# Issuing the end of attention's last block in steps within the next image's scans

## The chip, the cores and the metric

The kernel runs on one core of a Trainium2 chip. The metric is the device time of one execution in microseconds (us), lower is better; the time given is the median of several runs. A profile is one execution recorded by the hardware profiler; times in its views are us from the start of its span.

## The reference

Four images of 48 x 48 tokens with 128 channels go through two layers, each added to its input. All is float32.

```
x = x + ssm(groupnorm(x))          # layer 0: 2-D selective scan
t = tokens(x)                      # 2304 tokens of 128 channels
t = t + attention(layernorm(t))    # softmax(t t^T) t
t = t + stu(layernorm(t))          # spectral filters, 16 of them
```

Layer 0 projects each token to 256 channels and a gate, convolves them 3 x 3, and runs a linear recurrence over the tokens in four directions, with 16 states to a channel:

```
dA = exp(dt * A);  h = h * dA + (dt * u) * B;  y = sum_n h * C
```

The four y are summed, normalised, gated and projected back. Attention follows: scores, exponential, weighted sum, division by the sum of weights. The last part ("stu") is a causal convolution of the normalised tokens with 16 filters, at four lengths, mixed by weights, with a projection for each filter.

## The kernel before

**Phases.** The program does one image after the other (the loop at L1121). For image b it runs `scans` (the recurrence of b), then `epilogue` (normalise, gate, project: the input T of attention), then `attention`. The stu part of image b is not done there: it is the generator `stu`, which is drawn in small pieces inside the scans of image b + 1, and alone at the end for the last image. Likewise the prologue of image b + 1 and the first pieces of its scans' preparation (`begin_scans`) are drawn inside the attention of image b.

**Order.** Every engine (PE, DVE, ACT, POOL, and SP for DMAs) works its instructions in the order in which the Python code issues them; the order is written out by hand with generators that yield between steps. Tiles come from pools with a fixed number of buffers, and a tile that reuses a buffer waits for the last use of the former.

**Scans.** An image's recurrence has 24 chunks (4 directions by 6 stretches of 384 tokens), each with 8 units (2 halves of the channels by 4 groups of states). A unit's state tile s (pool of 6) holds 4 groups of 384 columns. For each unit: PE spreads B into a PSUM bank (L442); DVE multiplies it with rep, the loaded dt·u, into s (L450; for three units of eight POOL does this, with a loaded row of B, `bc`); ACT forms dA and DVE scans, four times (L455, L458); POOL copies the carry (L466) and multiplies by C, also a `bc` row (L467); PE sums over the states into the bank y (L475), and DVE adds that to the image's sum. In `scans` the steps of neighbouring units are interleaved: `enter`, `spread`, `prepare` (a step of a later chunk's preparation), `scan`, and `more`, which draws stu pieces until their columns keep pace.

**DMA at the turning.** `begin_scans` issues on SP, during the attention of the image before, the first chunk's dtdud stores, its rep loads (L402) and its six `bc` rows of four pieces each (L429). stu then issues, at its first draw, four filter tiles `tt` (L942), and for each of its five blocks of rows ux (L1001, L1002), mue (L1004), `res`, the tokens to which the result is added (L1006, from the tensor td), and G (L953) for each filter. ACT takes the first two `cv` results of a filter by a copy to Q (L983).

**Attention.** Blocks of queries J are taken in the order 0, 4, 1, 2, 3 (L698). For each block, 18 tiles of keys: scores on PE (L714), exponential on ACT (L716), values on PE into the bank o (L707). When a block is complete, its `tail` begins, a generator in steps:

- DVE copies o to oT (L857); PE turns it (otr, L861);
- DVE forms the denominators (den, L864 to L867) and adds the result to T (L871, L872);
- SP stores T to the tensor td in DRAM (L874);
- the layer norm of stu, `normed`: DVE sum, mean and difference (L151 to L153), ACT square (L154), DVE variance (L156, L157), POOL power (L158), DVE product into u (L160), and us from u (L886);
- PE turns u (utr, L890), ACT copies it to uT (L893), SP stores that to the tensor ud (L895).

One step of the oldest tail is taken per tile of keys. After the last tile of the last block, what is left is run to its end at once:

```
        while es:
            values()
        for t in tails:
            for _ in t:
                pass
```

The driver then closes attention's pools, opens those of the next scans, and calls `scans`.

Of the kernel before, what the change touches and what calls it, by code (L numbers as in the profile page):

```python
# [8 lines left out]
F32 = mybir.dt.float32  # L9
# [6 lines left out]
P = 128  # L16
B, H, W, C = 4, 48, 48, 128
# [4 lines left out]
CS = 384  # L22
SUB = 384
NT = L // P
# [30 lines left out]
def hybrid_kernel(ctx: ExitStack, tc: tile.TileContext, a: dict, out: bass.AP):  # L55
# [453 lines left out]
    def scans(b, chunks, preps, front, sp, back, work, work_cols):  # L509

        units = [Unit(ch, h, q) for ch in chunks for h, q in quads]
        total = len(chunks) * CHUNK_COLS + work_cols
        done = [0]

        def more(share):

            while done[0] < share * total:
                cols = next(work, None)
                if cols is None:
                    break  # L520
                done[0] += cols

        def enter(s):

            if s + 2 < len(units) and units[s + 2].pool:
                units[s + 2].enter(sp.s)
            if 0 <= s + 1 < len(units) and not units[s + 1].pool:
                units[s + 1].enter(sp.s)

        def spread(s):  # L530
            if s < len(units) and not units[s].pool:
                units[s].spread(back.psB)
                done[0] += CS

        def prepare(s):

            ci, j = divmod(s, len(quads))
            for c in range(ci + 1, ci + 4):
                if c < len(chunks) and 0 <= s - len(quads) * c + LEAD < STEPS:
                    done[0] += next(preps[c]) or 0  # L540

        def refill(s, i):

            if 0 <= s < len(units) and s // len(quads) + 1 < len(chunks):
                u, nxt = units[s], chunks[s // len(quads) + 1]
                if u.h == NH - 1:
                    nxt.fetch(i + u.q, front)

        pending = []
        spread(0)  # L550
        enter(-2)
        enter(-1)
        spread(1)
        for s in range(len(units) + 2):
            real = s < len(units)
            enter(s)
            prepare(s)
            if real:
                units[s].scan(0, back.psa)
            more((s + 0.25) / len(units))  # L560
            if 1 <= s <= len(units):
                units[s - 1].times_c()
            if real:
                units[s].scan(1, back.psa)
            if pending:
                pending.pop().add_y()
            prepare(s)
            more((s + 0.5) / len(units))
            spread(s + 2)
            if real:  # L570
                units[s].scan(2, back.psa)
            more((s + 0.75) / len(units))
            prepare(s)
            if real:
                units[s].scan(3, back.psa)
            refill(s - 3, Q4)
            if s + 1 < len(units) and units[s + 1].pool:
                refill(s + 1, 0)
            if s >= 2:
                units[s - 2].sum_c(back.psy)  # L580
                done[0] += CS
                if units[s - 2].q == Q4 - 1:
                    pending.append(units[s - 2])
            more((s + 1) / len(units))
        for u in pending:
            u.add_y()
        assert next(work, None) is None
# [3 lines left out]
    def epilogue(b, T, xn, xnT, tmp, pool, ps):  # L591
# [13 lines left out]
        def load_z(J):  # L605
            n = P * PIECES[J]
            zr[J] = tmp.tile([P, NH, 512], F32, tag=f"zr{J}", name=f"zr{b}_{J}")
            nc.sync.dma_start(zr[J][:, :, :n], zs[:, :, at(J)].rearrange("h p t -> p h t"))
            nc.sync.dma_start(T[:, 4 * J:4 * J + PIECES[J]], tokens(a["x"][b], J))

        def means(J):
            n = P * PIECES[J]
# [40 lines left out]
        def add(J, j0):  # L653
            if j0 >= PIECES[J]:
                return
            p = o.pop((J, j0))
            for f in range(2):
                t = T[:, 4 * J + j0 + f]
                nc.vector.scalar_tensor_tensor(t, p[:, 0, f], rd[J][:, j0 + f:j0 + f + 1], t, ALU.mult, ALU.add)
            t = T[:, 4 * J + j0:4 * J + j0 + 2]  # L660
            nc.vector.tensor_tensor(t, t, p[:, 1], ALU.add)

        def norm(J):
            if J not in lns:
                n = PIECES[J]
                sq = pool.two.tile([P, 4, C], F32, tag="ln_sq", name=f"asq{b}_{J}")[:, :n]
                lns[J] = normed(T[:, 4 * J:4 * J + n], xn[:, 4 * J:4 * J + n], 1e-5, pool.two, sq, f"a{b}_{J}")
            next(lns[J], None)

        def turned(J):  # L670
# [15 lines left out]
                    stage(slot - s)  # L686
                    yield slot - s if stage is kept else None

    def attention(b, T, xn, xnT, pool, tmp, ps):

# [2 lines left out]

        pieces = [0, 4, 1, 2, 3]  # L698
        slots = [(J, i) for J in pieces for i in range(NT)]
        es, po, tails = [], {}, []  # L700

        def values():
            J, i, e = es.pop(0)
            w = P * PIECES[J]
            if i == 0:
                po[J] = ps.two.tile([P, 512], F32, tag="o", name=f"o{b}_{J}")
            nc.tensor.matmul(po[J][:, :w], xn[:, i], e[:, :w], start=(i == 0), stop=(i == NT - 1))  # L707
            if i == NT - 1:
                tails.append(tail(b, J, T, po.pop(J), tmp, ps))

        for J, i in slots:
            w = P * PIECES[J]
# [9 lines left out]
            yield  # L722
        while es:
            values()
        for t in tails:
            for _ in t:
                pass
# [119 lines left out]
        for t in us[b]:  # L847
            nc.gpsimd.memset(t[KP[-1]:, NM - 1], 0.0)

    def tail(b, J, T, po, pool, ps):  # L850


        u, sums = us[b]
        n, k = PIECES[J], KP[J]
        T = T[:, 4 * J:4 * J + n]
        oT = pool.two.tile([P, 512], F32, tag="oT", name=f"oT{b}_{J}")
        nc.vector.tensor_copy(oT[:, :P * n], po[:, :P * n])  # L857
        yield
        p = ps.two.tile([P, 4, C], F32, tag="tr", name=f"otr{b}_{J}")[:, :n]
        for j in range(n):  # L860
            nc.tensor.transpose(p[:, j], oT[:, j * P:(j + 1) * P], ident)  # L861
        yield
# [11 lines left out]
        nc.sync.dma_start(tokens(td, J), T)  # L874
        x = T
        if n < 4:

# [2 lines left out]
            nc.sync.dma_start(x[:k], td[512 * J:].rearrange("(p j) c -> p j c", j=4))  # L880
            for i in range(3):
                yield
        sq = pool.one.tile([P, 4, C], F32, tag="sq", name=f"usq{b}_{J}")
        for _ in normed(x[:k], u[:k, J], 1e-5, pool.two, sq, f"u{b}_{J}"):
            yield
        nc.vector.tensor_tensor(sums[:k, J], u[:k, J, 0:2], u[:k, J, 2:4], ALU.add)  # L886
        yield
        p = ps.two.tile([P, 512], F32, tag="tr", name=f"utr{b}_{J}")[:, :4 * k]
# [3 lines left out]
        uT = pool.two.tile([P, 4 * P], F32, tag="uT", name=f"uT{b}_{J}")[:, :4 * k]  # L892
        nc.scalar.copy(uT, p)  # L893
        yield
        nc.sync.dma_start(ud[:, :, 1 + P * J:1 + P * J + k], uT.rearrange("c (j p) -> c j p", j=4))  # L895
# [4 lines left out]
    def stu(b, pool, ps):  # L900
# [95 lines left out]
        def begin(n):  # L996
            (lo, hi, place, extra), k = items[n]
            m = 2 if extra else 1

            now["x"] = pool.one.tile([P, 6, P], F32, tag="ux", name=f"ux{b}_{n}")  # L1000
            nc.sync.dma_start(now["x"][:, 2:, :hi - lo], ud[:, :, 1 + lo:1 + hi])  # L1001
            nc.sync.dma_start(now["x"][:, :2, :hi - lo], ud[:, 2:, lo:hi])  # L1002
            now["mu"] = pool.one.tile([P, 2, 3, C], F32, tag="mue", name=f"mue{b}_{n}")
            nc.sync.dma_start(now["mu"][:, :m], mud[:, place:place + m])  # L1004
            now["T", n] = pool.two.tile([P, 4, C], F32, tag="res", name=f"res{b}_{n}")
            nc.sync.dma_start(now["T", n][:hi - lo], td[4 * lo:4 * hi].rearrange("(p j) c -> p j c", j=4))  # L1006

        def parts(w, extra):

# [40 lines left out]
            yield 4 * w  # L1050

        def ended(n, p, lo, hi):
            t = now.pop(("T", n - KF + 1))[:hi - lo]
# [4 lines left out]
        for n, (_, k) in enumerate(items):  # L1058
            if k == 0:
                begin(n)  # L1060
            for c in range(3):
                for g in range(2):
                    yield from conv(n, c, g)
# [54 lines left out]
    first = begun(begin_scans(0, front))  # L1118
    begin0.close()
    start_y(0)  # L1120
    for b in range(B):  # L1121
        sp = Stage(tc, f"h{b}", "left", s=(6, SB))
        ps = Stage(tc, f"b{b}", "right", psa=(2, PSUM), psy=(1, PSUM), psB=(1, PSUM), psc=(3, PSUM), psp=(1, PSUM))
        bank["mm"] = ps.psB, "B"
        if b == 0:
            mixed = Stage(tc, "m", "right", two=(2, SB))
            scans(b, *first, front, sp, ps, mixture(mixed, ps), MIX_COLS)
            mixed.close()
        else:
            scans(b, *first, front, sp, ps, stu_alone(b - 1, ps), STU_COLS)  # L1130
        ps.close()
        sp.close()
        front.close()
        turn = Stage(tc, f"t{b}", "left", one=(1, SB))
        back = Stage(tc, f"a{b}", "right", one=(1, SB), two=(2, SB), four=(4, SB))
        T = back.one.tile([P, NT, C], F32, tag="T", name=f"T{b}")
        xn = back.one.tile([P, NT, C], F32, tag="xn", name=f"xn{b}")
        xnT = back.one.tile([P, L], F32, tag="xnT", name=f"xnT{b}")
        begin_stu(b)
# [4 lines left out]
        at = attention(b, T, xn, xnT, back, back, ps)  # L1144
# [85 lines left out]
```

## Time and profile before

| | |
|---|---|
| time, 3 runs | 6412.86, 6416.79, 6426.66 us; median 6416.79 |
| span of the profile | 6421.2 us, 75575 instructions |
| mean granted TensorE clock | 0.919 |
| PE, DVE, ACT, POOL busy | 85%, 75%, 44%, 60% |
| DMA | 1033.52 MB, mean 161 GB/s |
| attention of image 0 to scans of image 1: last `o` copied, first scan, first `cv` | 1450.73, 1471.49, 1473.78 us |
| the same, images 1 to 2 | 2887.72, 2908.48, 2910.63 us |
| the same, images 2 to 3 | 4317.93, 4338.69, 4340.76 us |

How to read it: the busy shares are averages over phases with different limits, so what happens at one place has to be read from the timeline there. A line in the timeline gives start, duration, engine, line of the kernel, operation, the tiles written and read, and in brackets how long the engine had been idle and what ended that.

### The profile page before, as it was taken

Reading aid. Unit: us, or ns where it says so; the run is one execution under the profiler, and the core shown is the slowest. Engines: PE = TensorE matmul, PEld = TensorE weight load, DVE = VectorE, ACT = ScalarE, POOL = GpSimd, SP = SyncE. Lnnn points to the kernel's source line nnn. Section 1 sums busy time; section 2 is a strip of 40 time slices with the busy share of each in tenths; the row PEclk is TensorE's granted clock in tenths of the full one; section 3 lists DMA queues with packets and bytes.
Section 4 is the critical chain, followed back from the end, with each engine's and each line's share of the span. In section 5 each row is a group of like instructions: output and inputs, shape, how many; then the busy total and the mean of one; then the engine's idle time right before and its main releaser. Section 6 shows DMA issues by size and latency. Waiting matters only on the chain.

```text
span 6421.2 us, 75575 instructions
## 1 busy us (share of the span) xinstructions
PE 5440.6 (85%) x25032; PEld 3353.1 (52%) x25032; DVE 4823.6 (75%) x6193; ACT 2800.0 (44%) x5053; POOL 3842.7 (60%) x1825
## 2 busy tenths in 40 slices
PE   3656555697999998888999999788999999789999
PEld 1222222444556566544556567544555567547789
DVE  6999999548999998558999998458999999322111
ACT  2555555244555554244555554244555554221000
POOL 1989888406778887306788887207788888100000
PEclk6787777799999999899999999899999999899999
DMA  4556566126878889127878889127788888025546
GB/s 104 139 138 151 139 144 148 40 55 162 199 196 215 216 221 247 59 62 165 198 195 217 222 218 256 39 64 179 189 203 215 219 224 246 28 67 151 154 141 212
DMA packets 658246, 1033.52 MB, mean 161 GB/s; under 512 B 93856, under 2 KB 515872, under 8 KB 633120
## 3 DMA queue, kind: packets, MB, share of 16 engines
q1 hardware_dynamic: 652032, 1025.00, 62.3%
q10 hardware_dynamic: 5824, 3.69, 0.3%
q8 instruction: 200, 3.28, 0.2%
q14 instruction: 190, 1.56, 0.1%
HBM read 905.79 MB, written 122.56 MB: 160 GB/s over the span
## 4 chain that ended last, share of the span: by engine, by line
PE 45%; DVE 24%; DMA 16%; POOL 4%; issue 4%; ACT 4%; SPq 3%; DVEq 0%; ACTq 0%; POOLq 0%
PE cv L969 19%; DVE s L458 11%; PE pr L1031 6%; DVE s L450 5%; DMA tt<-fd 5%; DMA rep<-dtdud 4%; PE s L714 4%; PE y L475 3%; PE o L707 3%; DMA bc<-xdd 3%; POOL s L467 3%; PE op L650 2%; PE B L442 2%; DVE xc L264 2%; DVE re L408 2%
## 5 line engine op out<-in xcount | busy, mean ns | idle before, releaser
L467 POOL TENSOR_TENSOR s<-s,bc 128x1536 f32<-128x1536 f32 x768 | 2647.8, 3449 | 179.8 <-DVE s L458 88.9
L458 DVE TENSOR_TENSOR_SCAN s<-dA,carry,s 128x384 f32<-128x384 f32 x2560 | 2458.1, 1000 | 190.1 <-ACT dA L455 189.0
L455 ACT ACTIVATE dA<-rep,A 128x384 f32<-128x384 f32 x3072 | 1782.0, 585 | 1627.0 <-DVE s L458 1622.2
L969 PE MATMUL cv<-tt,u 128*128 128x256 f32 (+3 forms) x7680 | 1632.6, 351 | 64.3 <-DVE U L994 38.0
L969 PEld LDWEIGHTS cv<-tt,u 128*128 128x128 f32 x7680 | 1259.7, 190 | 583.1 <-issue 266.1
L450 POOL TENSOR_TENSOR s<-rep,bc 128x1536 f32<-128x1536 f32 x288 | 994.2, 3452 | 95.3 <-DMA bc<-xdd 95.3
L969 PE MATMUL cv<-tt,us 128*128 128x256 f32 (+3 forms) x3840 | 841.0, 358 | 106.6 <-DVE U L994 55.3
L994 DVE TENSOR_TENSOR U<-cv,Q 128x256 f32<-128x256 f32 (+1 forms) x1280 | 480.3, 381 | 596.0 <-PE cv L969 581.2
L450 DVE TENSOR_TENSOR s<-rep,B 128x1536 f32<-128x1536 f32 x480 | 832.2, 1734 | 56.1 <-PE B L442 32.8
L475 PE MATMUL y<-s,csum 128*32 128x384 f32 x6144 | 720.6, 544 | 142.4 <-DVE ya L481 85.0
L969 PEld LDWEIGHTS cv<-tt,us 128*128 128x128 f32 x3840 | 639.7, 195 | 323.8 <-DVE U L994 89.7
L1031 PE MATMUL pr<-U,G 128*128 128x512 f32 (+4 forms) x2048 | 694.7, 469 | 3.5 <-DVE U L994 3.2
L983 ACT COPY Q<-cv 128x256 f32<-128x256 f32 (+3 forms) x640 | 224.0, 351 | 1027.2 <-PE cv L969 1025.5
L442 PE MATMUL B<-xd,spread 128*128 128x384 f32 x960 | 443.0, 546 | 177.4 <-DVE s L450 166.8
L458 DVE TENSOR_TENSOR_SCAN s<-dA,s 128x384 f32<-128x384 f32 x512 | 459.3, 938 | 70.9 <-ACT dA L455 70.7
L466 POOL COPY carry<-s 128x4 f32<-128x4 f32 x640 | 121.6, 190 | 574.8 <-DVE s L458 534.5
L1031 PEld LDWEIGHTS pr<-U,G 128*128 128x128 f32 x2048 | 334.5, 190 | 198.2 <-issue 137.0
L714 PE MATMUL s<-xnT 128*128 128x512 f32 (+1 forms) x720 | 357.9, 582 | 42.7 <-ACT xnT L676 23.4
L475 PEld LDWEIGHTS y<-s,csum 128*32 128x32 f32 x6144 | 127.7, 112 | 497.4 <-issue 336.3
L158 POOL TENSOR_TENSOR ln_vu<-ln_vu,mhalf 128x4 f32<-128x4 f32 (+1 forms) x20 | 26.8, 1341 | 602.0 <-DVE ln_vu L157 602.0
L716 ACT ACTIVATE e<-s,shift 128x512 f32<-128x512 f32 (+1 forms) x360 | 231.2, 644 | 314.1 <-PE s L714 313.6
L707 PE MATMUL o<-e,xn 128*128 128x512 f32 (+1 forms) x720 | 343.4, 560 | 4.5 <-ACT e L716 4.5
(157 smaller groups left out, 3638.1 us busy)
## 6 DMA issues: line engine op xcount, KB each, us to landing
rep<-dtdud SPq DMA_DIRECT2D x768, 384.0 KB, 7.8
tt<-fd SPq DMA_DIRECT2D x192, 577.0 KB, 5.5
bc<-xdd SPq DMA_DIRECT2D x2304, 48.0 KB, 3.4
tt<-fd SPq DMA_DIRECT2D x192, 513.0 KB, 4.5
tt<-fd SPq DMA_DIRECT2D x192, 385.0 KB, 4.3
dtdud<-re SPq DMA_DIRECT2D x768, 96.0 KB, 2.3
G<-gd SPq DMA_DIRECT2D x192, 256.0 KB, 5.3
tt<-fd SPq DMA_DIRECT2D x64, 514.0 KB, 5.6
```

Source lines behind the costliest of these rows:

```text
L442: nc.tensor.matmul(self.bt[:, :CS], spread[:, self.ch.k // 2, self.q].rearrange("p c j -> p (c j)"), self.ch.xd, start=True, stop=True)
L450: eng.tensor_tensor(s, self.ch.rep[self.h][:, 1], bt.unsqueeze(1).to_broadcast([P, G4, CS]), ALU.mult)
L455: nc.scalar.activation(dA[:, :CS], ch.rep[self.h][:, 0, g], AF.Exp, scale=A[:, ch.k, self.h * G4 + g, self.q:self.q + 1])
L458: nc.vector.tensor_tensor_scan(s, dA[:, CS - 1::-1] if ch.rev else dA[:, :CS], s, 0.0 if ch.first else carry[:, self.h, self.q, g:g + 1], ...
L467: nc.gpsimd.tensor_tensor(self.s, self.s, ch.bc[Q4 + self.q].unsqueeze(1).to_broadcast([P, G4, CS]), ALU.mult)
L475: nc.tensor.matmul(ch.y[g * DL:(g + 1) * DL, :CS], csum, self.s[:, g], start=(self.q == 0), stop=(self.q == Q4 - 1))
L707: nc.tensor.matmul(po[J][:, :w], xn[:, i], e[:, :w], start=(i == 0), stop=(i == NT - 1))
L714: nc.tensor.matmul(p[:, :w], xnT[:, i * P:(i + 1) * P], xnT[:, 512 * J:512 * J + w], start=True, stop=True)
L716: nc.scalar.activation(e[:, :w], p[:, :w], AF.Exp, bias=shift)
L969: nc.tensor.matmul(p2[:, :, at - first:], x, t[:, :, hi - 1 - at + J * P:end if end >= 0 else None:-1], start=(J == 0), stop=(J == nb - 1))
L994: nc.vector.tensor_tensor(dst, src, q, ALU.add)
L1031: nc.tensor.matmul(p[:, :, :v], Gs[n][:, q, x, :], U[n][:, 4 * q:4 * q + 4, :v], start=False, stop=(k == KF - 1 and q == 1 and v == w))
```

## The change

The last block of attention (J = 3) of each image but the last keeps its tail as a generator. Only its first step, the copy to oT, is issued within attention. The others are issued from within `scans` of the next image by `attend()`: one ahead of the first `spread`, two after the first scan of unit 0, and then one at a time up to the middle of unit 2. Such a tail uses the bank y for its two transposes, and a tile of the state pool as scratch for the square and for uT; its small tiles lie in a pool that stays open. T of that block lies in the slot of u that the norm will fill. Its store to td is issued by ACT in place of SP, in a step of its own. T is one tile per block in place of one for all; `begin_stu`, which takes the tiles u and us and clears their last rows, comes ahead of the other tiles. In stu, `res` is loaded at the block's fourth filter (k = 3) in place of the first, and has one buffer in place of two.

```
+        def attend(n=1):
+            for i in range(n):
+                if last_tail and next(last_tail[0], True):
+                    last_tail.pop()
+
+        if last_tail:
+            bank["scratch"] = sp.s.tile([P, G4, CS], F32, tag="s", name=f"sc{chunks[0].name}").rearrange("p g t -> p (g t)")
+        attend()
         spread(0)
         enter(-2)
         enter(-1)
         spread(1)
...
                 units[s].scan(0, back.psa)
+            attend(2 if s == 0 else 1)
             more((s + 0.25) / len(units))
...
             prepare(s)
+            attend()
             more((s + 0.5) / len(units))
             spread(s + 2)
             if real:
                 units[s].scan(2, back.psa)
+            if s:
+                attend()
             more((s + 0.75) / len(units))
...
+            if s == 0:
+                attend()
             more((s + 1) / len(units))
```

```
         while es:
             values()
+        if rest is not None:
+            last_tail.append(tails.pop())
+            next(last_tail[0])
         for t in tails:
             for _ in t:
                 pass
...
-        nc.sync.dma_start(tokens(td, J), T)
+        (nc.scalar if scratch else nc.sync).dma_start(tokens(td, J), T)
+        if scratch:
+            yield
...
-        sq = pool.one.tile([P, 4, C], F32, tag="sq", name=f"usq{b}_{J}")
+        if scratch:
+            sq = bank["scratch"][:, :4 * C].rearrange("p (j c) -> p j c", c=C)
+        else:
+            sq = pool.one.tile([P, 4, C], F32, tag="sq", name=f"usq{b}_{J}")
...
-            now["T", n] = pool.two.tile([P, 4, C], F32, tag="res", name=f"res{b}_{n}")
-            nc.sync.dma_start(now["T", n][:hi - lo], td[4 * lo:4 * hi].rearrange("(p j) c -> p j c", j=4))
+
+        def load_T(n):
+            (lo, hi, place, extra), k = items[n]
+            now["T"] = pool.one.tile([P, 4, C], F32, tag="res", name=f"res{b}_{n}")
+            nc.sync.dma_start(now["T"][:hi - lo], td[4 * lo:4 * hi].rearrange("(p j) c -> p j c", j=4))
...
             if k == 0:
                 begin(n)
+            elif k == 3:
+                load_T(n)
...
+        rest = Stage(tc, f"r{b}", "right", one=(1, SB), two=(1, SB)) if b + 1 < B else None
+        begin_stu(b)
...
-        T = back.one.tile([P, NT, C], F32, tag="T", name=f"T{b}")
+
+        T = [us[b][0][:, J] if rest and J == PIECE_ORDER[-1] else
+             back.one.tile([P, n, C], F32, tag=f"T{J}", name=f"T{b}_{J}") for J, n in enumerate(PIECES)]
```

More of the change, by code (lines that the diff above doesn't have):

```diff
@@ L549, in scans, with attend @@
         pending = []
+        def attend(n=1):
+            for i in range(n):
+                if last_tail and next(last_tail[0], True):
+                    last_tail.pop()
+        if last_tail:
+            bank["scratch"] = sp.s.tile([P, G4, CS], F32, tag="s", name=f"sc{chunks[0].name}").rearrange("p g t -> p (g t)")
+        attend()
         spread(0)
@@ L559, in scans @@
                 units[s].scan(0, back.psa)
+            attend(2 if s == 0 else 1)
             more((s + 0.25) / len(units))
@@ L567, in scans @@
             prepare(s)
+            attend()
             more((s + 0.5) / len(units))
@@ L571, in scans @@
                 units[s].scan(2, back.psa)
+            if s:
+                attend()
             more((s + 0.75) / len(units))
@@ L583, in scans @@
                     pending.append(units[s - 2])
+            if s == 0:
+                attend()
             more((s + 1) / len(units))
@@ L608, in load_z @@
             nc.sync.dma_start(zr[J][:, :, :n], zs[:, :, at(J)].rearrange("h p t -> p h t"))
-            nc.sync.dma_start(T[:, 4 * J:4 * J + PIECES[J]], tokens(a["x"][b], J))
+            nc.sync.dma_start(T[J], tokens(a["x"][b], J))
         def means(J):
@@ L657, in add @@
             for f in range(2):
-                t = T[:, 4 * J + j0 + f]
+                t = T[J][:, j0 + f]
                 nc.vector.scalar_tensor_tensor(t, p[:, 0, f], rd[J][:, j0 + f:j0 + f + 1], t, ALU.mult, ALU.add)
-            t = T[:, 4 * J + j0:4 * J + j0 + 2]
+            t = T[J][:, j0:j0 + 2]
             nc.vector.tensor_tensor(t, t, p[:, 1], ALU.add)
@@ L666, in norm @@
                 sq = pool.two.tile([P, 4, C], F32, tag="ln_sq", name=f"asq{b}_{J}")[:, :n]
-                lns[J] = normed(T[:, 4 * J:4 * J + n], xn[:, 4 * J:4 * J + n], 1e-5, pool.two, sq, f"a{b}_{J}")
+                lns[J] = normed(T[J], xn[:, 4 * J:4 * J + n], 1e-5, pool.two, sq, f"a{b}_{J}")
             next(lns[J], None)
@@ L687, in epilogue, with attention @@
                     yield slot - s if stage is kept else None
-    def attention(b, T, xn, xnT, pool, tmp, ps):
-        pieces = [0, 4, 1, 2, 3]
+    def attention(b, T, xn, xnT, pool, tmp, ps, rest):
+        pieces = PIECE_ORDER
         slots = [(J, i) for J in pieces for i in range(NT)]
@@ L708, in values @@
             if i == NT - 1:
-                tails.append(tail(b, J, T, po.pop(J), tmp, ps))
+                kept_ = rest is not None and J == pieces[-1]
+                tails.append(tail(b, J, T[J], po.pop(J), rest if kept_ else tmp,
+                                  last_bank if kept_ else lambda name: ps.two.tile([P, 512], F32, tag="tr", name=name), kept_))
         for J, i in slots:
@@ L848, in begin_stu, with last_bank, tail @@
             nc.gpsimd.memset(t[KP[-1]:, NM - 1], 0.0)
-    def tail(b, J, T, po, pool, ps):
+    PIECE_ORDER = [0, 4, 1, 2, 3]
+    last_tail = []
+    def last_bank(name):
+        pool, tag = bank["tail"]
+        return pool.tile([P, 512], F32, tag=tag, name=name)
+    def tail(b, J, T, po, pool, mm_tile, scratch):
         u, sums = us[b]
         n, k = PIECES[J], KP[J]
-        T = T[:, 4 * J:4 * J + n]
         oT = pool.two.tile([P, 512], F32, tag="oT", name=f"oT{b}_{J}")
@@ L858, in tail @@
         yield
-        p = ps.two.tile([P, 4, C], F32, tag="tr", name=f"otr{b}_{J}")[:, :n]
+        p = mm_tile(f"otr{b}_{J}").rearrange("p (j c) -> p j c", c=C)[:, :n]
         for j in range(n):
@@ L887, in tail @@
         yield
-        p = ps.two.tile([P, 512], F32, tag="tr", name=f"utr{b}_{J}")[:, :4 * k]
+        p = mm_tile(f"utr{b}_{J}")[:, :4 * k]
         for j in range(4):
@@ L891, in tail @@
         yield
-        uT = pool.two.tile([P, 4 * P], F32, tag="uT", name=f"uT{b}_{J}")[:, :4 * k]
+        uT = (bank["scratch"] if scratch else pool.two.tile([P, 4 * P], F32, tag="uT", name=f"uT{b}_{J}"))[:, :4 * k]
         nc.scalar.copy(uT, p)
@@ L1052, in ended @@
         def ended(n, p, lo, hi):
-            t = now.pop(("T", n - KF + 1))[:hi - lo]
+            t = now["T"][:hi - lo]
             nc.vector.tensor_tensor(t, t, p[:hi - lo], ALU.add)
@@ L1120, in hybrid_kernel @@
     start_y(0)
+    rest = None
     for b in range(B):
@@ L1124, in hybrid_kernel @@
         bank["mm"] = ps.psB, "B"
+        bank["tail"] = ps.psy, "y"
         if b == 0:
@@ L1130, in hybrid_kernel @@
             scans(b, *first, front, sp, ps, stu_alone(b - 1, ps), STU_COLS)
+        assert not last_tail
         ps.close()
@@ L1133, in hybrid_kernel @@
         front.close()
+        if rest:
+            rest.close()
+        rest = Stage(tc, f"r{b}", "right", one=(1, SB), two=(1, SB)) if b + 1 < B else None
+        begin_stu(b)
         turn = Stage(tc, f"t{b}", "left", one=(1, SB))
         back = Stage(tc, f"a{b}", "right", one=(1, SB), two=(2, SB), four=(4, SB))
-        T = back.one.tile([P, NT, C], F32, tag="T", name=f"T{b}")
+        T = [us[b][0][:, J] if rest and J == PIECE_ORDER[-1] else
+             back.one.tile([P, n, C], F32, tag=f"T{J}", name=f"T{b}_{J}") for J, n in enumerate(PIECES)]
         xn = back.one.tile([P, NT, C], F32, tag="xn", name=f"xn{b}")
         xnT = back.one.tile([P, L], F32, tag="xnT", name=f"xnT{b}")
-        begin_stu(b)
         more = b + 1 < B
@@ L1143, in hybrid_kernel @@
         bank["mm"] = ps.one, "mm"
-        at = attention(b, T, xn, xnT, back, back, ps)
+        at = attention(b, T, xn, xnT, back, back, ps, rest)
         slots = NT * len(PIECES)
```

## The prediction

> **What bounds the kernel now.** I read the page first: the tenths of each engine, then the chain. No engine binds everywhere; the chain runs through PE for 45% and DVE for 24%.
>
> ```profile
> PE   3656555697999998888999999788999999789999
> DVE  6999999548999998558999998458999999322111
> ...
> PE 45%; DVE 24%; DMA 16%; POOL 4%; issue 4%; ACT 4%; SPq 3%; DVEq 0%; ACTq 0%; POOLq 0%
> ```
>
> So I went to the place of the change. There are three turnings from an image's attention to the next image's scans. In the timeline of the first (columns: start, us, engine, line) everything after the last `o` matmul hangs on one serial thread:
>
> ```profile
> 1450.73 0.68 DVE L857 COPY oT<-o 128x512 f32<-128x512 f32 x1
> 1451.47 0.65 PE L861 MATMUL otr<-ident,oT 128*128 128x128 f32 x4 [1.19 <-DVE oT L857]
> ...
> 1454.44 0.34 SPq L874 DMA_DIRECT2D td<-T  x1
> ...
> 1458.77 3.42 POOL L450 TENSOR_TENSOR s<-rep,bc 128x1536 f32<-128x1536 f32 x1
> 1458.83 3.90 DVE L160 TENSOR_TENSOR u<-u,ln_vu 128x512 f32<-128x512 f32 x1 [1.19 <-POOL ln_vu L158]
> ...
> 1464.64 1.65 PE L442 MATMUL B<-xd,spread 128*128 128x384 f32 x2 [0.68 <-ACT uT L893]
> 1466.32 1.75 DVE L450 TENSOR_TENSOR s<-rep,B 128x1536 f32<-128x1536 f32 x1 [3.13 <-PE B L442]
> ...
> 1468.16 4.17 SPq L942 DMA_DIRECT2D tt<-fd  x4
> ...
> 1471.49 1.80 DVE L458 TENSOR_TENSOR_SCAN s<-dA,s 128x384 f32<-128x384 f32 x2
> ...
> 1473.78 2.08 PE L969 MATMUL cv<-tt,us 128*128 128x256 f32 x4 [4.01 <-DMA tt<-fd]
> ...
> 1475.04 0.37 ACT L983 COPY Q<-cv 128x256 f32<-128x256 f32 x1 [9.47 <-PE cv L969]
> ```
>
> Call the start of oT O. The first scan comes at O+20.8 and the first `cv` at O+23.05; in the second and third turning (O at 2887.72 and 4317.93) the first `cv` is at O+22.9 and O+22.8. Two threads start the scans: the tail with B and the state products, and SP's queue, which must bring `tt` before ACT's Q copy, behind which the third dA waits. So SP's queue and what it waits for (us, times, longest) come next:
>
> ```profile
> 1428.25 20.68 SPq L429 DMA_DIRECT2D bc<-xdd  x24
> ...
> 1449.70 0.57 SPq L386 DMA_DIRECT2D xdd<-xd  x1
> ```
> ```profile
> SPq L429 <- DMA rep<-dtdud: 11.3, 8, 1.6
> ```
> ```profile
> 4308.81 7.75 SPq L429 DMA_DIRECT2D bc<-xdd  x17
> ```
>
> A bc load shares no data with rep, yet waits for it eight times. [...] Freed of rep (the third turning), 17 pieces take 7.75 us, 0.456 each.
>
> [...] L160 takes 3.90 us beside POOL's 3.42 us L450, with a median of 0.693 otherwise. [...] here a B takes 1.65 us after the tail against 0.81 later.
>
> **The change, part by part.**
>
> *Taken out.* The tail from otr to the ud store no longer stands ahead of B. If nothing else moved, PE would do otr at O+0.74 to 1.39, then B 0.85, product 1.75, B 0.85, product 1.75 with handovers of about 0.05: first scan at O+6.75, 14.0 us earlier.
>
> *The wait put in.* The td store moves from SP to ACT. The changed kernel, built but not run, shows its order and waits, the same at all three turnings:
>
> ```
> ACT  td<-u             waits DVE (T done), DMAHW0
> SP   bc row 3, piece 1 waits DMAHW6
> SP   bc row 3, piece 2 waits DMAHW7
> SP   bc row 3, piece 3 waits DMAHW0
> ```
>
> The value that piece 3 waits for on DMAHW0 is reached only when ACT's td has landed. [...] SP, which passed these pieces from 1433 on, now stops at the seventh. Behind it on SP: 18 bc pieces, block 2's ud store, xdd, four dtdud, then `tt`, ux and mue; waiting for them are POOL's products, PE's first `cv`, and through Q all later dA and scans.
>
> When td lands: first scan O+6.75 to 7.7; den, four operations, 1.06 us (1452.16 to 1453.22) and T, five operations, 1.2 (to 1454.41): O+9.95. ACT's issue and landing aren't in the trace for td; SP's td lands in 1.7 to 2.5 us, median 2.0, and ACT's only comparable issue row is 0.59 us long. I take 2.2 with the handover, and 0.35 for B's that are partly slow (0 to 0.84 each): td lands at O+12.5 (11.8 to 14.3).
>
> Then SP: 18 pieces at 0.456 are 8.2 us (7.0 at 0.39, which is 20.68 less the 11.3 waited, over 24; 11.9 at 0.66, halfway to the 0.86 beside rep, which has long landed by then). ud and xdd 0.66 each with gaps, four dtdud 2.6 with gaps: 4.0. `tt` goes out at O+24.7, against O+17.4 before; with the same 5.65 us to the first `cv` it comes at O+30.3: **7.4 us later than before** (5.4 to 12).
>
> *Added to DVE within the first two units.* den and T lie ahead of td and are in the sum; the Q wait hides nothing more of them. The rest stands between the fourth scan of unit 0 and the third of unit 1: L151 0.72, L152 0.20, L153 0.71, L156 0.72, L157 0.20, L160 0.70, L886 0.45 with gaps: 3.7 us. The new pow on POOL is followed by a carry copy and a 3.45 us L467 product; [...] one of them is likely to sit behind it: 3.3 us (0 to 3.3). DVE had 3.4 us idle there before (the first scan of unit 2 waits for dA at 1488.05, because ACT waits for xd, xp, pr and mue). So that scan comes at +7.4+3.7+3.3−3.4 = +11.0, while PE, which must do utr after L160, is at +8.5 (+7.4, plus L151 to L160, 3.3 with gaps, less the 2.2 it waited for mue at 1481.37). DVE has idle shares behind this point (busy 9.44 of 10 from 1490 to 1500), so I let the difference close mostly: **+9 us per turning**.
>
> *Costed at nothing, each hidden by:* otr's four transposes (PE waits for O anyway); utr's and uT (0.6 us each, counted in PE's lag); the new wait of L153 for td's landing (landed 20 us before); the ud store from the scratch tile on SP, which waits for uT and has rep x4 of the second chunk behind it (issued at 1481.91 before, now some 17 us later, still landing, at 9.1 us, more than 10 us ahead of the scan at 1525 plus the delay); unit 4's state taking the scratch tile's buffer (two units later than the store); y's first sum (after uT). T in five tiles and block 3's in u's slot: the loads wait for the same end of the spectral filter. The memsets keep their place on POOL. `res` at k = 3 and in one buffer: 20 issues of 0.43 us move on SP; the stores they wait for were issued two or more filters earlier, and `res` doesn't stand in the chain. Dropping it from the start of a block could give mue up to 1 us, 0 to 5 in all; I take 0.
>
> *Sum.* Three turnings of +9: +27 us, on the profile's span of 6421.2. The runs shown are 6412.86 to 6426.66, median 6416.79; I put the difference on the median: **6444 us**. The bounds per turning are +3 (quick store, pieces at 0.39, [...] some later idle used up) and +15 (the slow ends): +9 to +45.
>
> **Rivals.**
>
> 1. *SP isn't held* (the other side). If piece 3 doesn't wait for td, SP has done xdd at 1450.3 and `tt` goes out near O+2.2; the first scan is 14.0 earlier, den and T put 2.3 back, the other DVE work 3.6 net of the idle: −8.1 per turning, −24 in all, 6393. It decides at one place: whether bc's 24 pieces run through from 1428 to 1449. For it: the tail's data need no bc. Against it: the wait in the built order, and the eight waits on rep[...]. It holds too if the steps do just what the change says.
> 2. *Held, but mostly made good.* DVE's scans wait 259.7 us for dA over the whole run; if the first chunk swallows the added work and catches up, +3 per turning: 6426, within what can't be told apart. For it: DVE's idle shares in the first units. Against: PE and DVE go in lockstep at 9 tenths after 1490.
> 3. *Held, with more behind it.* The late `tt`, ux, mue and dtdud crowd rep of the second chunk, whose load lands late; +15 per turning: 6462. For it: DMA busy share is 0.96 from 1470 to 1490. Against: the slack of over 10 us counted above.
>
> **How the numbers follow.** A measurement of this kernel tells about 0.2% (12.8 us) from no change: 6404 to 6430. My forecast (held, +5 to +13 per turning) has 0.72, rival 3 0.10, rival 2 0.10, rival 1 0.08. So slower 0.82, same 0.10, faster 0.08. The forecast and rival 3's nearer part lie within 6424 to 6462; what is left out is rival 1, part of 2 and of 3.
>
> **What would show it.** Right: SP's bc<-xdd broken after six pieces until td lands, near O+12.5; first scan near O+7, but the first `cv` near O+30; a long ACT wait before Q; L160 or L886 at about 3.9 us. Wrong: bc unbroken, first `cv` before O+15, or a DVE that has caught up by unit 8 of the first chunk.

## The result, and the profile after

| | before | after |
|---|---|---|
| time, median of 4 runs | 6414.82 us (6405.95 to 6426.66) | 6452.49 us (6450.70 to 6455.69) |
| ratio | | 1.0058, 95% interval 1.0041 to 1.0076 |
| span of the profile | 6421.2 us | 6449.9 us |
| first scan after the copy to oT, first turning | O+20.8 | O+7.2 |
| `tt` issued | O+17.4 | O+24.9 |
| first `cv` | O+23.05 | O+30.9 |

The change made the kernel 0.6% slower: 37.7 us by the medians, 12.6 a turning (a turning is the passage from one image's attention to the next one's scans; there are three). In the changed kernel's numbering oT is L885, the td store L902, `us` L919, ud L928, `tt` L975, `cv` L1002, Q L1016.

The timeline of the changed kernel at the first turning (start, us, engine, line; O is 1449.13; SPq and ACTq are the queues on which SP and ACT issue DMAs):

```profile
1449.13 0.68 DVE L885 COPY oT<-o 128x512 f32<-128x512 f32 x1
...
1456.37 0.95 DVE L458 TENSOR_TENSOR_SCAN s<-dA,s 128x384 f32<-128x384 f32 x1
...
1459.49 0.33 ACTq L902 DMA_DIRECT2D td<-u  x1
1461.51 8.19 SPq L429 DMA_DIRECT2D bc<-xdd  x18
1464.00 3.42 POOL L450 TENSOR_TENSOR s<-rep,bc 128x1536 f32<-128x1536 f32 x1 [39.97 <-DMA bc<-xdd]
...
1474.03 4.37 SPq L975 DMA_DIRECT2D tt<-fd  x4
...
1480.04 2.08 PE L1002 MATMUL cv<-tt,us 128*128 128x256 f32 x4 [25.38 <-DMA tt<-fd]
...
1481.35 0.37 ACT L1016 COPY Q<-cv 128x256 f32<-128x256 f32 x1 [32.88 <-PE cv L1002]
...
1483.05 0.96 DVE L458 TENSOR_TENSOR_SCAN s<-dA,s 128x384 f32<-128x384 f32 x1 [22.73 <-ACT dA L455]
...
1491.97 3.79 POOL L467 TENSOR_TENSOR s<-s,bc 128x1536 f32<-128x1536 f32 x1
1492.51 3.54 DVE L919 TENSOR_TENSOR us<-u 128x256 f32<-128x256 f32 x1
...
1493.44 1.04 PE L1002 MATMUL cv<-tt,us 128*128 128x256 f32 x4
1495.97 2.64 DVE L458 TENSOR_TENSOR_SCAN s<-dA,s 128x384 f32<-128x384 f32 x3
1496.95 0.58 ACT L455 ACTIVATE dA<-rep,A 128x384 f32<-128x384 f32 x1 [3.16 <-DVE s L458]
...
1497.94 0.65 ACT L1016 COPY Q<-cv 128x256 f32<-128x256 f32 x2
...
1498.37 0.70 PE L1002 MATMUL cv<-tt,u 128*128 128x256 f32 x2 [3.89 <-ACT Q L1016]
```

The first scan does come 13.5 us earlier. But 18 pieces of bc start only 2.0 us after ACT has issued td, though SP had passed them by 1449 in the kernel before. I call this stop of SP the hold. POOL has stood idle for 40 us when they let its first product start, PE 25 us when `tt` lets it start the first `cv`, ACT 33 us when it gets that `cv`, and DVE, two scans into unit 0, waits 22.7 us for ACT. SP's waits in the same stretch (us, times, longest) name what held it:

```profile
SPq L429 <- DMA td<-u: 23.6, 1, 23.6
```

On the page of the changed kernel the same shows as idle time (last column: us, what ended most of it). The rows are POOL's product with a bc row and PE's first `cv` group; before, they waited 95.3 us (bc) and 106.6 us:

```profile
L450 POOL TENSOR_TENSOR s<-rep,bc 128x1536 f32<-128x1536 f32 x288 | 994.2, 3452 | 213.7 <-DMA bc<-xdd 212.5
...
L1002 PE MATMUL cv<-tt,us 128*128 128x256 f32 (+3 forms) x3840 | 839.2, 357 | 161.6 <-DMA tt<-fd 100.0
```

**A measure for each turning.** To follow a delay further than the first units, I use the start of the first scan of unit 15 (the second chunk's last), counted from O, in the timelines. Before, it is at O+117.39, 117.17 and 116.48 in the three turnings; in the changed kernel at O+130.13, 130.64 and 129.59: 12.7, 13.5 and 13.1 later, 39.3 in all. That accounts for the 37.7 us of the medians. The scan in the first turning, before and changed:

```profile
1568.12 1.01 DVE L458 TENSOR_TENSOR_SCAN s<-dA,carry,s 128x384 f32<-128x384 f32 x1
```
```profile
1579.26 1.01 DVE L458 TENSOR_TENSOR_SCAN s<-dA,carry,s 128x384 f32<-128x384 f32 x1
```

The table gives the same for all kernels. The experiments ran in three groups; each time is beside the median of before on the same chip (6414.37, 6415.45 and 6414.71 us).

| kernel | `tt` issued, first turning | unit 15 against before, three turnings | sum | median, us | less its before | ratio, 95% interval |
|---|---|---|---|---|---|---|
| changed | O+24.9 | +12.7, +13.5, +13.1 | +39.3 | 6452.49 | +37.7 | 1.0058 (1.0041 to 1.0076) |
| e1_td_sp | O+10.8 | -0.8, -0.4, +0.1 | -1.2 | 6418.19 | +3.8 | 1.0006 (0.9999 to 1.0012) |
| e2_before_td_act | O+19.4 | +4.0, +0.3, +1.2 | +5.5 | 6413.08 | -1.3 | 1.0001 (0.9993 to 1.001) |
| e3_us_pool | O+24.9 | +6.8, +7.0, +7.3 | +21.1 | 6430.73 | +16.4 | 1.0023 (1.0014 to 1.0032) |
| e5_td_sp_us_pool | O+10.8 | -7.2, -6.6, -6.1 | -19.9 | 6394.57 | -20.9 | 0.9968 (0.9957 to 0.998) |
| e6_td_pool | O+2.6 | -7.2, -6.8, -6.2 | -20.2 | 6389.28 | -26.2 | 0.9959 (0.9946 to 0.9971) |
| e7_td_pool_us_pool | O+2.5 | -13.6, -7.6, -12.4 | -33.6 | 6384.12 | -31.3 | 0.9948 (0.9935 to 0.9962) |
| e8_td_act_later | O+2.7 | -7.0, -6.9, -6.2 | -20.1 | 6388.76 | -26.7 | 0.9962 (0.995 to 0.9975) |
| e9_us_reduce | O+2.6 | -10.4, -10.0, -9.9 | -30.3 | 6378.57 | -36.1 | 0.9946 (0.9934 to 0.9959) |
| e10_td_act_later_us_pool | O+2.7 | -11.2, -10.6, -12.1 | -33.9 | 6379.59 | -35.1 | 0.9947 (0.9933 to 0.996) |

The sums and the measured differences agree within 7 us, so the large differences arise for the most part in the three turnings; for e1 and e2 even the signs disagree, and the small difference in time says nothing there. e4_before_res is not in the table; its three turnings add up to -0.4.

### The profile page after: what moved, and what is told of

It reads as the page before. It is cut to its first block, busy times and chain, and to the rows that moved or that the text cites. A ratio compares the mean times of both kernels' runs of the same rounds, so it can differ in the third digit from the quotient of the medians.

```text
span 6449.9 us, 75574 instructions
## 1 busy us (share of the span) xinstructions
PE 5455.0 (85%) x25032; PEld 3364.2 (52%) x25032; DVE 4822.8 (75%) x6193; ACT 2799.4 (43%) x5053; POOL 3843.4 (60%) x1825
## 4 chain that ended last, share of the span: by engine, by line
PE 46%; DVE 23%; DMA 17%; issue 5%; POOL 3%; ACT 3%; SPq 3%; DVEq 0%; ACTq 0%; POOLq 0%
PE cv L1002 20%; DVE s L458 10%; PE pr L1067 6%; DMA tt<-fd 6%; DVE s L450 5%; DMA rep<-dtdud 5%; PE s L732 4%; PE y L475 3%; PE o L723 3%; DMA bc<-xdd 3%; POOL s L467 2%; PE op L665 2%; PE B L442 2%; DVE xc L264 2%; DVE re L408 2%
## 5 line engine op out<-in xcount | busy, mean ns | idle before, releaser
L1002 PE MATMUL cv<-tt,u 128*128 128x256 f32 (+3 forms) x7680 | 1638.4, 352 | 74.1 <-DVE U L1027 38.0
L1002 PEld LDWEIGHTS cv<-tt,u 128*128 128x128 f32 x7680 | 1264.0, 191 | 594.1 <-issue 270.5
L1002 PE MATMUL cv<-tt,us 128*128 128x256 f32 (+3 forms) x3840 | 839.2, 357 | 161.6 <-DMA tt<-fd 100.0
L1002 PEld LDWEIGHTS cv<-tt,us 128*128 128x128 f32 x3840 | 637.0, 194 | 375.4 <-DVE U L1027 93.8
L1016 ACT COPY Q<-cv 128x256 f32<-128x256 f32 (+3 forms) x640 | 224.0, 351 | 1083.3 <-PE cv L1002 1081.3
```

The lines of the kernel that those rows point to most:

```text
L1002: nc.tensor.matmul(p2[:, :, at - first:], x, t[:, :, hi - 1 - at + J * P:end if end >= 0 else None:-1], start=(J == 0), stop=(J == nb - 1))
```

## The experiments

The theory: in the built program the td store, moved to ACT, has its turn ahead of 18 bc pieces, and SP stood until td had landed (23.6 us in the view above). By turn I mean a transfer's place in the order in which the built program counts transfers on the semaphores named DMAHW; the expectation of e8 calls that order the rotation. The theory's rivals: the cost is ACT's issue or the added work on DVE, the store's traffic, or the other edits of the change (`res`).

**e1_td_sp: the store back on SP.**

```
-        (nc.scalar if scratch else nc.sync).dma_start(tokens(td, J), T)
+        nc.sync.dma_start(tokens(td, J), T)
```

> The changed kernel with one edit: the last block's store of T to td goes back to SP's queue, where it stands after xdd and four dtdud and ahead of tt. Theory [...]: the 24 bc pieces run through before the turning; td goes out when T is done, near O+10 (O is the start of oT of block 3), tt just after it, first cv near O+16 instead of O+30.9; the added DVE work [...] cost 3.6 us a turning net of idle; so about 3.4 us a turning less than the kernel before, some 10 us: about 6405 us where the kernel before has 6415. Rival (the steps' own work on DVE[...] and the new layout are the loss): bc may run through, but the time stays at least 10 us above the kernel before.

The hold is gone and the time falls 34 us from the changed kernel's, to that of before. It didn't fall to 6405. SP's waits and its timeline (two views) are as they were expected:

```profile
SPq L902 <- DVE u L900: 7.8, 1, 7.8
```
```profile
1457.04 0.35 SPq L902 DMA_DIRECT2D td<-u  x1
1457.48 4.02 SPq L975 DMA_DIRECT2D tt<-fd  x4
```

The store waits for T in SP's own order, and `tt` is behind it, at O+10.8; the first `cv` is at O+16.5. The miss lies behind that. The first scan of unit 1 is 5.0 us earlier than before, that of unit 3 only 1.0 and that of unit 15 only 0.8 (first turning): the added work on DVE took more than the 3.6 us estimated for it. e5 shows what it was. The late store held SP from either queue: 23.6 us from ACT's, and 7.8 us from SP's own, where it stands behind bc and not ahead of it.

**e2_before_td_act: in the kernel before, only the store of block 3 on ACT.**

```
-        nc.sync.dma_start(tokens(td, J), T)
+        (nc.scalar if J == 3 and b + 1 < B else nc.sync).dma_start(tokens(td, J), T)
```

> The kernel before with one edit: the last block's store of T to td is issued by ACT instead of SP (images 0 to 2). [...] though the tail is where it was, SP stops at the sixth of the 24 bc pieces (row 3, piece 2) for some 22 us until td has landed, near O+5.8. Then 19 pieces (8.7 us), two stores (1.3), the last ud store and four dtdud (3.3) put tt at about O+19, 1.7 us later than before: +5 us in all, at most +10. L160 falls from 3.90 to 0.69 us, since POOL's product waits for bc row 3 and no longer starts beside it. Rival (the queue doesn't matter, only where the steps stand): SP's bc pieces run through as before and the time is unchanged.

SP's waits, and SP's timeline:

```profile
SPq L429 <- DMA td<-T: 18.0, 1, 18.0
```
```profile
1429.07 34.32 SPq L429 DMA_DIRECT2D bc<-xdd  x24
...
1468.44 4.32 SPq L942 DMA_DIRECT2D tt<-fd  x4
```

The move alone makes the hold: bc takes 34.32 us and not 20.68. Yet the time is that of before. There the tail is still ahead of the scans, so T is ready earlier, `tt` slips by only 2 us, and POOL's first product, which has to wait 0.84 us for its bc row, starts only behind L160 (1457.90 against 1457.10). So L160 falls from 3.90 to 0.69 us, and the first scan is at O+17.55. The late `tt` then takes that gain back: the first scan behind Q is at O+27.85, against O+26.07. The hold cost less here, with another thread nearly as late: at unit 8 the kernel is 4.1, 2.0 and 2.8 us behind before. In the second and third turning some 1.7 us of that come back further on, from the clock (see e3), and what is left can't be told from nothing in the time.

**e3_us_pool: in the changed kernel, the sum `us` of the last block on POOL.**

```
-        nc.vector.tensor_tensor(sums[:k, J], u[:k, J, 0:2], u[:k, J, 2:4], ALU.add)
+        (nc.gpsimd if scratch else nc.vector).tensor_tensor(sums[:k, J], u[:k, J, 0:2], u[:k, J, 2:4], ALU.add)
```

> The changed kernel with one edit: for the last block, us is formed by POOL instead of DVE, right after POOL's power and product order[...]. Theory: the 3.54 us that us takes on DVE at each turning go; PE stands at +8.5 us a turning and DVE at +11, so 1 to 3.5 us a turning come off, some 6 us in all: about 6446 where the changed kernel has 6452. SP's hold stays as it is (bc broken after six pieces). [...]

SP is held as in the changed kernel, yet 22 us are gone where 6 had been expected: 6 a turning at unit 15, where 1 to 3.5 had been counted. At the first scan of unit 3 the saving is 3.8 us (first turning), at that of unit 5 4.3. The rest, 1.6 us, comes between the first scans of units 9 and 12. There the windows of the two kernels hold the same work (PE, PEld, DVE, ACT, POOL busy, granted clock, DMA share, GB/s). The changed kernel:

```profile
1541.50:1560.00 18.50, 16.16 (x65) 8.57 (x66) 16.00 (x24) 8.28 (x17) 13.93 (x6) 0.91 0.73 168
```

e3_us_pool:

```profile
1537.30:1554.20 16.90, 14.55 (x65) 7.92 (x66) 16.01 (x24) 8.20 (x17) 13.95 (x6) 1.00 0.73 168
```

65 matmuls at a granted clock of 0.91 or 1.00: 1.6 us. The kernel before has the slow form too (18.55 us, 18.54 and 18.48 in its three turnings). Shorter windows in the changed kernel show that the 0.91 is a mean, with 0.50 in the middle of it:

```profile
1543.00:1545.00 2.00, 2.00 (x6) 1.27 (x7) 2.00 (x4) 0.14 (x1) 1.82 (x1) 0.80 0.05 10
1545.00:1547.00 2.00, 2.00 (x5) 1.01 (x3) 0.64 (x2) 0.65 (x2) 0.00 (x0) 0.50 0.77 169
1547.00:1549.00 2.00, 2.00 (x13) 1.00 (x13) 1.44 (x2) 2.00 (x5) 0.60 (x2) 0.84 0.87 222
```

In windows of 0.3 us the clock is 1.00 up to 1544.0, 0.50 from 1544.3 to 1547.6 and 1.00 again from 1547.9. The other two turnings of the changed kernel and the three of the kernel before have such a stretch at 0.50 too, each 3 us long or a little more; I call it the slow stretch. Just ahead, PE idles some 2.44 us for U in every turning of every trace, 36 in all:

```profile
1542.88 0.70 PE L1002 MATMUL cv<-tt,u 128*128 128x258 f32 x2 [2.44 <-DVE U L1027]
```

In 24 of these turnings a slow stretch follows, in the other 12 the clock stays at 1.00. What decides between the two was not shown. It is not the wait of `us` as such: e9 takes the wait away and has the slow stretch in all three turnings, e2 keeps `us` on DVE and has it in one only.

**e4_before_res: in the kernel before, only `res` at k = 3 and in one buffer.**

```
-            now["T", n] = pool.two.tile([P, 4, C], F32, tag="res", name=f"res{b}_{n}")
-            nc.sync.dma_start(now["T", n][:hi - lo], td[4 * lo:4 * hi].rearrange("(p j) c -> p j c", j=4))
...
+            elif k == 3:
+                load_T(n)
```

> The kernel before with one edit: res is loaded at the fourth filter of a block, in one buffer. Theory: nothing to be told apart, 0 to 5 us faster, because res stands in no chain and mue comes ahead of it on the queue. Rival (the single buffer or the later issue holds SP): slower by 5 us or more, with SP waiting at L1006 or its successor for the out store.

6414.32 us beside 6414.37: ratio 0.9999 (0.999 to 1.0007). In the kernel before, this part costs nothing that can be told apart.

**e5_td_sp_us_pool: e1 and e3 together.**

> The changed kernel with the last block's store of td back on SP (as in e1_td_sp) and the sum us of that block on POOL (as in e3_us_pool). Both causes named so far are taken away, the hold of SP's queue (worth 34 us in e1) and the sum's 3.5 us behind POOL's product (worth 22 us in e3, 7 a turning). Theory that the two add up: 3.5 to 7 a turning less than e1's 6418, so 6397 to 6408, faster than before by 0.1 to 0.3%. Rival, that after the hold is gone PE's or POOL's work sets the time in units 1 and 2 and the DVE's 3.5 us are slack there: 6418, as e1. In the trace the sum's row on DVE is gone, and the scan that followed it starts about O+29 and not O+32.5 (O the copy of oT).

6394.57 us: 24 less than e1, as e3 is 22 less than the changed kernel, and 2 under what was expected. The two causes add up; with both edits the change is 0.3% faster than before. Up to unit 5 taking `us` off DVE is worth 4.6 to 4.8 us a turning, which covers e1's miss of 3 a turning; another 1.6 a turning is the clock, as in e3: the four `xp` matmuls behind PE's 2.44 us of idle time take 2.18 us in e1 and 1.45 in e5 (first turning).

**e6_td_pool and e7_td_pool_us_pool: the store on POOL's queue; e7 with `us` on POOL too.**

```
-        (nc.scalar if scratch else nc.sync).dma_start(tokens(td, J), T)
+        (nc.gpsimd if scratch else nc.sync).dma_start(tokens(td, J), T)
```

> The changed kernel with the last block's store of td issued on POOL's queue and not on ACT's; in the built program it counts on another set of semaphores (DMASW0) than the stores and loads of SP, and the 24 pieces of bc keep the turns that they have in before. Theory [...]: the 24 pieces run through unbroken, nothing of the T update stands ahead of tt, so tt is issued by about O+3 (O+10.8 in e1, O+24.9 in the changed kernel), the first cv by O+9, the third scan by O+14 (19.5 in e1), and the time is 3 to 5 a turning under e1: 6403 to 6409. Rival A (it was td's traffic or its landing that slowed the bc pieces, not its turn): the 24 pieces still take over 30 us and the time stays at 6440 to 6452. Rival B (POOL waits for T with its products behind it): POOL's first product of unit 0 starts after O+15 and the time is 6418 or more.

> e6_td_pool with the sum us of the last block on POOL as well. If the two are independent, another 3.5 to 7 a turning under e6: 6385 to 6400, the fastest of all and 0.2 to 0.45% faster than before. If the stage is by then bound by PE's projections or POOL's products, as e6, about 6405.

In e6 bc takes 20.68 us unbroken, and `tt` goes out at O+2.6. Rival A falls: the store moves the same data at nearly the same time. Rival B falls as well; POOL's timeline (O is 1447.50) has its product directly behind the store, at O+11.4:

```profile
1458.15 0.78 POOL L902 DMA_DIRECT2D td<-u  x1 [35.75 <-DVE u L900]
1458.95 3.45 POOL L450 TENSOR_TENSOR s<-rep,bc 128x1536 f32<-128x1536 f32 x1
```

e6 came out 14 us under the lower end of its expectation, e7 just under that of its own. e7's second turning is the odd one: from unit 9 to unit 12 it took 19.9 us, with two slow stretches, and 16.9 in the other two turnings.

**e8_td_act_later: the store on ACT, one step later.** The same instruction on the same queue. Only the yield that stood behind it stands ahead of it:

```
-        (nc.scalar if scratch else nc.sync).dma_start(tokens(td, J), T)
         if scratch:
             yield
+        (nc.scalar if scratch else nc.sync).dma_start(tokens(td, J), T)
```

> The changed kernel with the store of td still on ACT's queue, but issued one step later (the yield that follows it stands before it): in the built program it then takes its turn in the rotation after tt, ux and mue and not ahead of the bc pieces, and the next SP transfer on its semaphore is ud of the same block. Same instruction, same queue, same data. Theory of the turn: SP is not held, bc's 24 pieces take about 20 us, tt is issued by about O+3, and the time falls to 6403 to 6412 (as e6). Rival (ACT's issue, the store's traffic or the added DVE work are the cost, and the turn is incidental): still 6440 or more. Between them: if tt comes early but the time stays over 6425, the hold was not what set the end.

6388.76 us, 64 under the changed kernel and 14 under the lower end of what was expected. SP's timeline, then that of all engines (O is 1447.79):

```profile
1425.38 20.75 SPq L429 DMA_DIRECT2D bc<-xdd  x24
```
```profile
1450.47 4.28 SPq L975 DMA_DIRECT2D tt<-fd  x4
...
1455.90 2.08 PE L1002 MATMUL cv<-tt,us 128*128 128x256 f32 x4 [2.58 <-DMA tt<-fd]
...
1459.03 0.33 ACTq L904 DMA_DIRECT2D td<-u  x1
...
1464.87 0.69 DVE L153 TENSOR_TENSOR u<-u,ln_su 128x512 f32<-128x512 f32 x1 [3.04 <-DMA td<-u]
...
1470.85 3.79 POOL L467 TENSOR_TENSOR s<-s,bc 128x1536 f32<-128x1536 f32 x1
1471.39 3.53 DVE L919 TENSOR_TENSOR us<-u 128x256 f32<-128x256 f32 x1
```

ACT issues the store at O+11.2, hardly later than in the changed kernel (O+10.4). But in the order in which the program was written it now comes after bc, `tt`, ux and mue, and SP's waits from 1415 to 1530 have none for td. So what made the kernel slower was the turn of the store, and neither ACT's issue, its traffic nor the added DVE work, which are all still there (the DVE work has a price of its own, see e9, but with it the kernel is faster than before). (The line L153 pays 3.0 us in this turning: it overwrites the tile that td is still being read from.)

**e9_us_reduce and e10_td_act_later_us_pool: e8 without the 3.5 us of the sum `us`.** e10 takes the edit of e3. e9 keeps the sum on DVE, in its place, but as an operation with one SBUF input:

```
+        if scratch:
+            nc.vector.tensor_reduce(sums[:k, J], u[:k, J].rearrange("p (i j) c -> p j c i", i=2), AX.X, ALU.add)
+        else:
+            nc.vector.tensor_tensor(sums[:k, J], u[:k, J, 0:2], u[:k, J, 2:4], ALU.add)
```

> e8_td_act_later, with the sum us of the last block still on DVE at the same place, but as a reduction over the pair, which reads one SBUF tensor, and not as an addition, which reads two. Theory [...]: the row takes about 0.7 us while POOL's L467 runs, the scan after it starts at about O+24 (O+27 in e8), and the time is 3.5 to 6 a turning under e8's 6388.8: 6370 to 6379, or at least as e7's 6384. Rival (the row waits for something else, or the DVE time is slack by then): it stays near 3.5 us, or the time stays at 6386 to 6392.

> e8_td_act_later with the sum us of the last block on POOL, as in e3, e5 and e7[...]. POOL adds an operation of about 1.2 us; e3 gained 22 us, e5 24, e7 5 by the same edit. By the scans' starts in those traces 4.5 to 6.5 a turning: 6370 to 6384. If POOL's added operation delays the products, a little more than e9.

The timeline of e9:

```profile
1473.19 3.79 POOL L467 TENSOR_TENSOR s<-s,bc 128x1536 f32<-128x1536 f32 x1
1473.72 0.70 DVE L920 TENSOR_REDUCE us<-u 128x256 f32<-128x512 f32 x1
```

Beside the same product of POOL the sum takes 0.70 us and not 3.53. So it had not waited for data or for its place on DVE; the time went with the form of the operation, an addition of two SBUF tensors in place of a reduction of one. What about the form decides was not shown. Nor does every two-input operation of DVE take longer there: in the kernel before, a product with one input from SBUF (rep) and one from PSUM (B) starts 0.23 us after the same product of POOL and takes 1.74 us, where the mean over the run is 1.73:

```profile
1479.26 3.45 POOL L467 TENSOR_TENSOR s<-s,bc 128x1536 f32<-128x1536 f32 x1
1479.49 1.74 DVE L450 TENSOR_TENSOR s<-rep,B 128x1536 f32<-128x1536 f32 x1
```

Both times are as expected: e9 and e10 (6378.57 and 6379.59) have the lowest medians, 0.53 to 0.54% under before; they can't be told apart, nor from e7. Against e8, e9 is 3.4 us a turning earlier at unit 15 with the same slow stretch: that is what the wait alone was worth there.

## Why the prediction was right, and where its sum was off

**Held SP: right.** Step by step, first turning, predicted and measured: first scan O+6.75 and 7.24; td landed O+12.5 and 12.4 (bc goes on); 18 pieces 8.2 and 8.19 us; `tt` O+24.7 and 24.9; first `cv` O+30.3 and 30.9; the first scan of unit 2 +11.0 and +11.2 against before (O+48.6 and O+37.3). One of the two named operations did sit behind POOL's product: the sum `us`, 3.54 us, while L160 took 0.69; the 3.3 us put on it were my estimate, from L160's 3.90 us against 0.693 in the kernel before. e8 isolates the cause: the hold costs 19.8 us a turning at unit 15 (13.1 and 6.7), and the rest of the change saves 6.7. Two sums in the working are slightly off and don't matter: the delay of the first `cv` comes to 7.3 by its own terms, not 7.4, and its upper end to 12.8, not 12.

**The first rival's number: right for a kernel that the change was not.** "SP isn't held" was put at 6393; e8, which is that case, has 6388.76, and -6.7 a turning at unit 15 where -8.1 was worked out. That the times agree so well is partly luck: 6.6 us of e8's gain lie outside the turnings.

**The term that was mis-sized: the closing at the end of the sum.** Its last step was: "so I let the difference close mostly: +9 us per turning". The time came out inside the range, but each turning, at 12.6 us, near the upper end of the +5 to +13 that was forecast. The term rested on PE, put at +8.5 while the scans were at +11.0. PE was there at first: `cv<-tt,us` of the next filter starts at 1493.44 (O+44.3), against O+36.0 before: +8.3. The same place in the kernel before (O is 1450.73):

```profile
1486.76 1.03 PE L969 MATMUL cv<-tt,us 128*128 128x256 f32 x4
...
1487.95 0.65 ACT L983 COPY Q<-cv 128x256 f32<-128x256 f32 x2
1488.05 0.96 DVE L458 TENSOR_TENSOR_SCAN s<-dA,s 128x384 f32<-128x384 f32 x1 [3.41 <-ACT dA L455]
...
1488.38 0.70 PE L969 MATMUL cv<-tt,u 128*128 128x256 f32 x2 [0.58 <-ACT Q L983]
```

But the next `cv` row of PE in the changed kernel, `cv<-tt,u` at 1498.37 (O+49.2, before O+37.7), is at +11.6. It waited 3.89 us for Q, which ACT had behind a dA that waited for DVE's scans, and these stood behind `us`. So DVE's 3.5 us went through ACT into PE, which I had counted on to close the gap: +11.2 at unit 2 (first turning) didn't close to +9 but became +12.8 at unit 5 and stayed there up to unit 15 (12.7, 13.5 and 13.1 in the three turnings). e3 shows that `us` is the cause: without it on DVE the delay at unit 5 is 8.5, 8.7 and 8.9. (At unit 15 it is 7.0, but there the clock has given back another 1.6.) The slow stretch isn't the reason for the difference from before, which has it too.

**Costed at nothing.** `res` at k = 3: confirmed by e4. The ud store ahead of rep of the second chunk: at 1498.07, with rep behind it at 1498.69. Unit 8 is the first that works on that rep, and its delay is that of unit 5 (12.8 us in the first turning, 13.5 and 13.1 in the others); so the late rep cost nothing that showed.

**Open.** What decides whether a slow stretch follows PE's idle time was not shown, and no experiment set it, so the 1.6 us a turning that go with it can't be counted on. What e6 and e8 gain outside the turnings, 6 us beyond their sums, was not followed; it is less than the spread of single runs. A version in which L153 writes to another tile was not run.

## What to carry to other kernels

When a transfer moves to another queue, ask not only what that queue has ahead of it but also which transfers of other queues wait for it in the built program. Here the store on ACT's queue, which waited for late data, held a bc piece on SP's queue for 23.6 us, and with it all that stood behind on that queue. The built order showed it, and one step later in the program turned a loss into a gain (from +38 to -27 us). The 3.5 us put on DVE were not absorbed by PE's slack either, because ACT between them carried them over (PE waited 3.89 us for Q). And where an edit gains more than the wait that it removes, look at the granted clock before giving all of it to the edit (in e3 1.6 of some 6 us a turning were the clock's).

## What the runs showed of the hardware

Three things I had not expected. In the changed kernel SP's bc pieces stood 23.6 us for a store that ACT issues; with the same store issued by POOL (e6) they ran unbroken for 20.68 us, and POOL spent 0.78 us on the issue (ACT 0.33). A DVE addition of two SBUF tensors took 3.53 us beside POOL's product, and 0.425 in the median of e8's blocks; the same sum as a reduction took 0.70 beside that product (e9). And an idle time of PE as short as 2.44 us was followed in 24 of 36 turnings by a stretch at a granted clock of 0.50 (1544.3 to 1547.6 in the changed kernel), and in 12 by none: the same 65 matmuls took 16.16 us of PE or 14.55.
